# A graph network on one core: the preparation written in another order, and the tables' first evictions moved to ScalarE

## The chip, the cores and the metric

The kernel runs on one core of a Trainium2 chip. The metric is the device time of one launch in microseconds (us); smaller is better. Times given as "the median of the runs" come from unprofiled launches, all others from one launch that the hardware profiler recorded.

## The reference

6250 nodes with 256 features each, and 100000 edges that are sorted by destination. The input is normalised row by row, clipped at zero, and goes through four layers. Each layer adds to every node the sum of the rows of its edges' sources, and then applies three dense maps. The input is added to the result.

```
h = maximum(layernorm(x), 0)
for l in range(3):
    s = h + segment_sum(h[src], dst, num_segments=6250)
    s = relu(s @ W1s[l] + b1s[l])
    s = relu(s @ W2s[l] + b2s[l])
    h = s @ W3s[l] + b3s[l]
s = h + segment_sum(h[src], dst, num_segments=6250)
s = relu(s @ cW1 + cb1); s = relu(s @ cW2 + cb2)      # 256 -> 64
return x + s @ cW3 + cb3
```

## The kernel before

**The main part.** Nodes are kept in 49 blocks of 128. For most pairs of blocks the sums over edges are done as matrix products: a table of edge counts (one byte per pair of nodes) is built once from one-hot matrices, kept in DRAM, and multiplied with the features of all nodes (`agg`, lines L1588 and L1665). The features lie in SBUF as `XY`, split in a high and a low half. For the other blocks of destinations the source rows are fetched one tile at a time (`rows<-table,idx`, L1382, on GpSimd's queue) and summed with small one-hot products (`sums`, L1419). The dense maps are in `mlp`. By linearity W1 is applied ahead of the sum, so that W3 of one layer and W1 of the next are fused into one matrix.

**The preparation** comes before all that and is what the change rewrites. It consists of three Python generators. Each `yield` ends a step, and the order in which the steps are drawn is the order in which each engine gets its instructions; nothing reorders them later. An engine that waits in one instruction holds everything behind it in its own queue.

- `look` finds where the edges of each half block (64 destinations, 98 of them, one to a partition) begin. It loads the first destination of every 128 edges, places each half block roughly (`half`, `at`), fetches a window of `NEAR` destinations for each (`near_i`, L663), and compares that window with 17 thresholds (`less`): 11 comparisons on VectorE (`junk`, L695), 6 on ScalarE (a `Sign` whose results are summed, L698). From `less` it gets the starting edge of every group of 4 destinations (`starts`) and queues 32 gathers of edges (`wd`, `ws`) in the list `asks`. A second, coarser search (`both`, `sel`, `spread`, `part`, L720 to L757) gives the edges of the blocks that are summed row by row, with 14 more gathers (`gd`, `gs`). Then come four rounds in which gathered edges become sources and columns (`hi`, `rel`, `f`, L773 to L779) and are transposed into `clT`, a check that the edges are sorted (`run`, `down`, L794), the flags `wrong`, and the final lists `idx` and `rel` (L826 to L845).
- `normed` normalises the input, two blocks to a step, with lags between its parts: statistics (`moments`, L879, six steps ahead), `scale` (`h`, ScalarE, L899), `turn` (transposes on TensorE, L908, copied to `ht` by ScalarE, L911), `times` (the product with W1, L920, one step after `turn`), `out` (`zs`, L932, every third on ScalarE, else on VectorE), `high` and `low` (`XY`, L936 on ScalarE and L940 on VectorE), `keep` (the store to the table in DRAM).
- `fused` makes the three fused matrices: transposes of W3 (L575, copied by ScalarE, L577), six products (L586, copied by L588), one store each. The bias row comes out of a product whose left side is `b3b`, a copy of the bias spread over 128 columns by GpSimd.

`ask(n)` issues up to `n` of the queued gathers on GpSimd; each waits for the last product of the current step. Before the change, all thresholds, all of `fused` and the coarse search are drawn first, and the steps of `normed` follow with the rest of `look` spread over them.

**After the preparation** the first 12 rounds of table building (`build`) run alone: VectorE makes two one-hot matrices (`lo` and `hi`, L1035), TensorE multiplies them (`bp`, L1076), and the result is evicted as bytes in two pieces, by ScalarE (L1084) and VectorE (L1086) in turn. Then the products of layer 0 start (L1588), fed with casts of the table (`a`, L1549), with the building of the other blocks between them.

## Time and profile before

| | before |
|---|---|
| median of 3 runs | 2129.72 us (2128.97 to 2136.23) |
| the profiled execution's own time | 2135.8 us |
| its span, first to last instruction | 2134.0 us |
| TensorE busy | 2057.4 us, 96% of the span |
| VectorE, ScalarE, GpSimd busy | 937.7, 864.3, 1445.4 us |
| first product of layer 0 starts | 142.70 us after the span's start |

In the views, PE is TensorE, DVE VectorE, ACT ScalarE, POOL GpSimd and SP the engine that issues most transfers; a name with a q (`ACTq`, `SPq`) is the engine's issuing of transfers. A row of a timeline has the start and the duration in us, the engine, the line, the operation, the tile written and the tiles read, the shapes, how often, and in brackets how long the engine stood idle before it and what ended that. A row of windows has, for one stretch of time, the busy time of each engine with its count of instructions, then the granted TensorE clock as a share of full speed, the share of the transfer engines in use, and GB/s.

### The profile page before, as it was taken

Reading aid. Unit: us, or ns where it says so; the run is one execution under the profiler, and the core shown is the slowest. Engines: PE = TensorE matmul, PEld = TensorE weight load, DVE = VectorE, ACT = ScalarE, POOL = GpSimd, SP = SyncE. Lnnn points to the kernel's source line nnn. Section 1 sums busy time; section 2 is a strip of 40 time slices with the busy share of each in tenths; the row PEclk is TensorE's granted clock in tenths of the full one; section 3 lists DMA queues with packets and bytes.
Section 4 is the critical chain, followed back from the end, with each engine's and each line's share of the span. In section 5 each row is a group of like instructions: output and inputs, shape, how many; then the busy total and the mean of one; then the engine's idle time right before and its main releaser. Section 6 shows DMA issues by size and latency. Waiting matters only on the chain.

```text
span 2134.0 us, 33393 instructions
## 1 busy us (share of the span) xinstructions
PE 2057.4 (96%) x12076; PEld 1487.8 (70%) x12076; DVE 937.7 (44%) x2192; ACT 864.3 (41%) x1775; POOL 1445.4 (68%) x1470
## 2 busy tenths in 40 slices
PE   4979999999999999999999999999999999999997
PEld 3756766667667777777776777777776777777675
DVE  7877867667673422222233322222233433333332
ACT  4856655556556522323232433222333432223231
POOL 2727777777774477777776377777776277777773
PEclk9979999999999999999999999999999999999999
DMA  5524545545455655455455554555456555556553
GB/s 157 176 98 139 162 142 153 158 140 164 150 158 152 213 163 155 153 181 164 142 186 167 173 160 148 173 165 169 146 168 195 170 172 181 184 180 194 183 160 119
DMA packets 184901, 347.61 MB, mean 163 GB/s; under 512 B 32446, under 2 KB 118496, under 8 KB 184726
## 3 DMA queue, kind: packets, MB, share of 16 engines
q0 software_dynamic: 68960, 185.41, 29.7%
q1 hardware_dynamic: 113838, 158.12, 22.3%
q8 instruction: 97, 1.59, 0.3%
q10 hardware_dynamic: 1928, 1.85, 0.3%
q14 instruction: 78, 0.64, 0.1%
HBM read 287.98 MB, written 57.26 MB: 162 GB/s over the span
## 4 chain that ended last, share of the span: by engine, by line
PE 88%; DVE 5%; DMA 4%; issue 1%; ACT 1%; POOL 1%; SPq 0%; DVEq 0%; POOLq 0%; ACTq 0%
PE agg L1665 43%; PE agg L1588 16%; PE sums L1419 11%; PE ps L1233 6%; PE ps L1290 6%; PE bp L1076 4%; DMA rows<-table,idx 3%; PE ps L1479 1%; POOL rows L1382 1%; DVE junk L695 1%; PE bp L920 1%; DVE hi L1035 1%; DVE at L1086 1%; PE ps L1245 0%; DMA table<-zs 0%
## 5 line engine op out<-in xcount | busy, mean ns | idle before, releaser
L1382 POOL DMA_INDIRECT rows<-table,idx x1394 | 1387.7, 995 | 611.4 <-issue 220.6
L1665 PE MATMUL agg<-a,XY 128*128 128x512 f32 x4116 | 982.8, 395 | 1.9 <-DVE clT L1600 1.9
L1665 PEld LDWEIGHTS agg<-a,XY 128*128 128x128 f32 x4116 | 764.6, 188 | 209.5 <-issue 45.8
L1565 ACT CAST a<-at 128x512 fp32r<-128x512 uint8 (+1 forms) x542 | 326.9, 616 | 576.9 <-PE agg L1665 543.9
L1565 DVE CAST a<-at 128x512 fp32r<-128x512 uint8 x543 | 242.7, 448 | 552.8 <-PE agg L1665 469.3
L1588 PE MATMUL agg<-XY,a 128*128 128x512 f32 x1470 | 404.9, 409 | 1.3 <-DVE un L1600 0.7
L1588 PEld LDWEIGHTS agg<-XY,a 128*128 128x128 f32 x1470 | 258.9, 189 | 53.7 <-issue 8.7
L1419 PE MATMUL sums<-rows,hot 128*32 128x256 f32 x3772 | 256.0, 385 | 16.2 <-DMA rows<-table,idx 15.0
L1419 PEld LDWEIGHTS sums<-rows,hot 128*32 128x32 f32 x3772 | 112.6, 109 | 142.6 <-issue 53.6
L1549 ACT CAST a<-at 128x512 fp32r<-128x512 uint8 (+2 forms) x362 | 196.7, 574 | 6.5 <-PE agg L1588 6.5
L1084 ACT CAST at<-bp 128x392 uint8<-128x392 f32 x240 | 116.6, 487 | 203.7 <-PE bp L1076 191.0
L1086 DVE CAST at<-bp 128x392 uint8<-128x392 f32 x240 | 135.1, 563 | 138.2 <-PE bp L1076 138.2
L1448 DVE TENSOR_TENSOR u<-u,sums 128x256 f32<-128x256 f32 x82 | 34.3, 419 | 241.8 <-PE agg L1665 226.9
L1076 PE MATMUL bp<-hi,lo 128*128 128x196 bf16 x960 | 127.5, 255 | 11.0 <-DVE hi L1035 10.7
L1290 PE MATMUL ps<-w,h 128*128 128x256 f32 x588 | 133.9, 379 | 1.4 <-ACT h L1236 0.9
L1233 PE MATMUL ps<-h,w 128*128 128x512 f32 (+3 forms) x332 | 133.9, 545 | 0.6 <-DVE zz L1298 0.6
L1035 DVE TENSOR_TENSOR hi<-cols,pairs 128x784 bf16<-128x784 bf16 x240 | 134.3, 560 | 0.0
L1076 PEld LDWEIGHTS <-lo 128*128 128x128 bf16 x960 | 70.6, 99 | 81.9 <-DVE hi L1035 27.8
L1290 PEld LDWEIGHTS ps<-w,h 128*128 128x128 f32 x588 | 111.1, 190 | 18.7 <-ACT h L1236 1.8
L1483 ACT ACTIVATE h<-ps,bias 128x256 f32<-128x256 f32 (+1 forms) x116 | 47.2, 464 | 154.9 <-PE ps L1479 154.9
L1298 DVE TENSOR_TENSOR zz<-ps,w 128x512 f32<-128x512 f32 (+1 forms) x75 | 50.1, 678 | 117.0 <-PE ps L1290 117.0
L1035 DVE TENSOR_TENSOR lo<-lanes,pairs 128x512 bf16<-128x512 bf16 x240 | 100.3, 418 | 1.3 <-ACT pairs L1030 1.3
(171 smaller groups left out, 989.7 us busy)
## 6 DMA issues: line engine op xcount, KB each, us to landing
at<-mat SPq DMA_DIRECT2D x151, 448.0 KB
mat<-at SPq DMA_DIRECT2D x30, 784.0 KB
rows<-table,idx POOLq DMA_INDIRECT x1394
table<-zz SPq DMA_DIRECT2D x72, 256.0 KB
back<-table SPq DMA_DIRECT2D x99, 128.0 KB
xs<-in_x_dram SPq DMA_DIRECT2D x8, 768.0 KB
table<-zs SPq DMA_DIRECT2D x24, 256.0 KB
out_dram<-zz SPq DMA_DIRECT2D x24, 256.0 KB
```

The lines of the kernel that those rows point to most:

```text
L1035: nc.vector.tensor_tensor(o.rearrange("p q (n t) -> p q n t", t=2), values.rearrange("p (n t) -> p n t", t=2)[:, None, :, :].to_broadcast( ...
L1076: mm = nc.tensor.matmul(bp[:, m * HW:(m + 1) * HW], lo[:, q + m, :], hi[:, q + m, :], start=True, stop=True)
L1084: nc.scalar.copy(o, v)
L1086: nc.vector.tensor_copy(o, v)
L1233: mm = nc.tensor.matmul(ps[:mp, :w], weights[l][0][:, c, i * P:i * P + mp], h1[:, c, :w], start=(c == 0), stop=(c == KC - 1))
L1290: mm = nc.tensor.matmul(o, h2[0][:, c, nodes], w3[:, c, :], start=(c == 0), stop=(c == KC - 1))
L1382: got = nc.gpsimd.indirect_dma_start(out=t, out_offset=None, in_=tables[self.l][:, :], in_offset=bass.IndirectOffsetOnAxis(ap=idx[:, o:o + ...
L1419: nc.tensor.matmul(self.sums[m * Q:(m + 1) * Q, :C], self.hot[:, (c - min(rounds)) // 2, m, :], self.rows[g, c + 4 * m], start=(c == ROUND ...
L1549: nc.scalar.copy(a[:, i * m * P:(i + 1) * m * P].rearrange("p (j d) -> p j d", j=m), counts[b][:, j:j + m, :])
L1565: cast(o, at[:, :, d:d + m * P])
L1588: mm = nc.tensor.matmul(agg, a[:, d:d + P], XY[:, j, :], start=(j == 0), stop=(j == NT - 1))
L1665: mm = nc.tensor.matmul(agg[c][:, :w], XY[:, j, o:o + P], a[:, :w], start=(j == 0 and half == 0), stop=(j == NT - 1 and half == 1))
```

## The change

The window `NEAR` shrinks from 1408 to 1280 destinations. Eight comparisons run on VectorE and nine on ScalarE, one or two of each kind in a step of `normed`; after each two such steps the function `settled` works out four groups' `starts` and queues their gathers. The statistics run four steps ahead instead of six, and only the first two of the four early loads of the input are issued ahead of the search. `fused` is drawn one step at a time beside `normed` and loads one layer's weights ahead; the bias is read as a broadcast operand, without `b3b`. The coarse search, its products, the flags and the last lists have steps of their own. In `build`, all evictions of the first 12 rounds are ScalarE's.

```diff
-    NEAR = 11 * P
+    NEAR = 10 * P
...
         load(0)
-        load(1)
         yield
         for l in range(NLAYER):
             w3, w1 = loaded[l]
+            load(l + 1)
...
-            b3b = pool.tile([P, KC, P], F32, name="b3b", bufs=1)
-            nc.gpsimd.tensor_copy(b3b, b3[l][:, :, None].to_broadcast([P, KC, P]))
...
-                    left = w3t[:, k, i * P:(i + 1) * P] if i < KC else b3b[:, k, :]
+                    left = (w3t[:, k, i * P:(i + 1) * P] if i < KC else
+                            b3[l][:, k:k + 1].to_broadcast([P, P]))
...
-        DV = 11
-        for q in range(GSUB + 1):
-            if q < DV:
-                nc.vector.tensor_scalar(junk[:NSUB], near[:NSUB], float(GD * q), None,
-                                        op0=OP.is_lt, op1=OP.add, accum_out=less[:NSUB, q:q + 1])
-            else:
-                nc.scalar.activation(junk2[:NSUB], near[:NSUB], AF.Sign, bias=edge[:NSUB, q:q + 1],
-                                     accum_out=less[:NSUB, q:q + 1])
-                yield
...
+        def settled(q0, q1):
+            odd = slice(q0 + 1 - q0 % 2, q1, 2) if q1 <= GSUB else slice(q0, q1)
+            nc.vector.tensor_scalar(less[:NSUB, odd], less[:NSUB, odd], -0.5, float(NEAR // 2),
+                                    op0=OP.mult, op1=OP.add)
+            nc.vector.tensor_scalar(first[:NSUB, q0:q1], less[:NSUB, q0:q1], at[:NSUB, 0:1], None,
+                                    op0=OP.add)
+            if q1 > GSUB:
+                return
+            nc.vector.tensor_scalar(starts[:, q0:q1], first[:NSUB, q0:q1], float(E - P), None,
+                                    op0=OP.min)
...
+        for q in range(0, GSUB, 2):
+            nc.vector.tensor_scalar(junk[:NSUB], near[:NSUB], float(GD * q), None,
+                                    op0=OP.is_lt, op1=OP.add, accum_out=less[:NSUB, q:q + 1])
+            for k in (q + 1,) if q + 2 < GSUB else (q + 1, q + 2):
+                nc.scalar.activation(junk2[:NSUB], near[:NSUB], AF.Sign, bias=edge[:NSUB, k:k + 1],
+                                     accum_out=less[:NSUB, k:k + 1])
+            yield
+            if q % 4 == 2:
+                settled(q - 2, q + 2)
+        settled(GSUB, GSUB + 1)
...
-        G = 6
+        G, LEAD = 6, 4
...
-            turn_biases()
-            for _ in range(2 * NLAYER):
-                next(looked)
-                next(ahead_w)
-            next(looked)
-            STAGES = (*range(4, 20, 2), 20, 22, 24)
+            STAGES = (*range(16), 17, *range(17, 28))
             for i, _ in enumerate(rows):
-                ask(2)
+                ask(3 if i < 9 else 2)
+                if i == 1:
+                    turn_biases()
+                if i < 2 * NLAYER + 1:
+                    next(ahead_w, None)
                 if i in STAGES:
                     next(looked, None)
...
-                    if step % 2:
+                    if step % 2 or step <= 2 * PRE:
                         nc.scalar.copy(o, v)
                     else:
                         nc.vector.tensor_copy(o, v)
```

Three places show how the instructions move. The first is ScalarE's queue from its first statistics on. Before, the comparisons (`near_i,less`) and the copies of the fused weights (`w3t`, `w_275`, `w_306`) come ahead of the first normalised rows `h`:

```order
L885 ACTIVATE std<-mv,eps 128x6 x2
L550 COPY bias<-ps 128x22
L698 ACTIVATE near_i,less<-near,edge 98x1408
L577 COPY w3t<-ps 128x256 x2
...
L588 COPY w_275<-ps 128x256 x3
...
L588 COPY w_306<-ps 128x256 x3
...
L588 COPY w_333<-ps 128x256 x3
L899 ACTIVATE h<-xs,shift,rstd 128x256 x4
```

In the changed kernel the same queue reads so; L898 is the statistics' root, L912 `scale`, L716 the comparison, L924 `turn`'s copy:

```order
L898 ACTIVATE std<-mv,eps 128x6
L912 ACTIVATE h<-xs,shift,rstd 128x256 x2
L527 DMA w_233<-in_L_gnn_W3s_dram 128x2x256
L527 DMA w1n<-in_L_gnn_W1s_dram 128x2x256
L577 COPY w3t<-ps 128x256 x2
L716 ACTIVATE near_i,less<-near,edge 98x1280
...
L924 COPY ht<-agg 128x512
...
L550 COPY bias<-ps 128x22
L587 COPY w_277<-ps 128x256 x3
```

The rows `h` have moved ahead of all comparisons, and one or two comparisons, one copy of a fused matrix and one pair of `h` now take turns. The second place is the end of the preparation on TensorE. Before, the transposes of the last lists (`wd`, `near`, L835) come ahead of the last transposes of the input and its last product (L920), and ten products into an unused bank (L926) close it:

```order
L920 MATMUL bp<-w_0_114,ht 128x256 x4
L835 MATMUL ps<-ident,wd 128x68 x6
L835 MATMUL ps<-ident,wd 128x17
L835 MATMUL ps<-ident,near 128x68 x6
L835 MATMUL ps<-ident,near 128x17
L908 MATMUL agg<-ident,h 128x128 x2
L920 MATMUL bp<-w_0_114,ht 128x256 x6
L926 MATMUL ps<-XY 128x512 x10
```

In the changed kernel L933 is `times`, L939 the ten products, and L848 the lists' transposes:

```order
L921 MATMUL agg<-ident,h 128x128 x2
L933 MATMUL bp<-w_0_114,ht 128x256 x6
L939 MATMUL ps<-XY 128x512 x10
L848 MATMUL ps<-ident,wd 128x68 x6
L848 MATMUL ps<-ident,wd 128x17
L848 MATMUL ps<-ident,near 128x68 x6
L848 MATMUL ps<-ident,near 128x17
```

The lists' transposes have gone behind all of the input's products. The third place is VectorE at the same end and the start of `build`. Before:

```order
L845 CAST idx<-ps 128x425
...
L932 COPY zs<-bp 128x512
...
L932 COPY zs<-bp 128x256
L940 TENSOR_TENSOR XY<-zs,XY 128x2x256
L940 TENSOR_TENSOR XY<-zs,XY 128x256
L1035 TENSOR_TENSOR lo<-lanes,pairs 128x512
L1035 TENSOR_TENSOR hi<-cols,pairs 128x784
...
L1086 CAST at<-bp 128x49x8
```

In the changed kernel, where L855 and L858 make the last lists, L945 is `out` and L953 `low`:

```order
L945 COPY zs<-bp 128x512
...
L855 TENSOR_SCALAR rel<-ps 128x25x4 x3
L858 CAST idx<-ps 128x425
L945 COPY zs<-bp 128x256
L953 TENSOR_TENSOR XY<-zs,XY 128x2x256
L953 TENSOR_TENSOR XY<-zs,XY 128x256
L1053 TENSOR_TENSOR lo<-lanes,pairs 128x512
L1053 TENSOR_TENSOR hi<-cols,pairs 128x784
```

The last lists, which stood ahead of two `zs`, now stand between the last full pair's `zs` and the last single block's, and in the first 12 rounds of `build` VectorE has only `lo` and `hi` (and one addition), without the `CAST`.

59 lines of the change are left out of this document (34 added, 25 removed).

## The prediction

> **What bounds the kernel now.** I read the page first, then windows over the first 143 us, then the timeline of each engine there. Rows of the page and of the windows:
>
> ```profile
> span 2134.0 us, 33393 instructions
> PE 88%; DVE 5%; DMA 4%; issue 1%; ACT 1%; POOL 1%; SPq 0%; DVEq 0%; POOLq 0%; ACTq 0%
> 0.00:15.20 15.20, 2.92 (x4) 0.96 (x4) 2.69 (x13) 0.00 (x0) 5.92 (x25) 1.00 0.73 221
> 15.20:42.90 27.70, 15.03 (x50) 10.82 (x50) 26.64 (x61) 15.36 (x30) 1.40 (x6) 0.94 0.38 122
> 42.90:66.60 23.70, 21.01 (x112) 16.41 (x111) 21.34 (x73) 17.55 (x38) 18.49 (x18) 0.93 0.55 164
> 66.60:111.70 45.10, 39.39 (x210) 31.12 (x208) 39.44 (x114) 37.19 (x84) 31.93 (x29) 1.00 0.53 158
> 111.70:125.80 14.10, 12.76 (x46) 10.13 (x46) 7.30 (x18) 4.62 (x10) 0.00 (x0) 0.64 0.24 82
> 125.80:142.70 16.90, 9.47 (x50) 5.14 (x50) 16.52 (x39) 7.08 (x18) 7.93 (x8) 0.59 0.45 150
> 200.00:300.00 100.00, 99.61 (x685) 68.94 (x684) 72.98 (x169) 61.12 (x138) 73.86 (x74) 1.00 0.47 142
> ```
>
> TensorE carries 88% of the chain, and in the sample from 200 to 300 us it is busy 99.61 of 100 us. The code there is unchanged (eviction alternates as before after round 12), so an earlier start of the products moves the end by as much. What the change can win or lose lies before 142.7 us. There VectorE is the third number of busy time: 26.64 of 27.70 us, later 39.44 of 45.10, and 16.52 of 16.90 in the first rounds of `build`. Its idle time up to 125.8 us is 125.8 less the 97.4 us that the first five windows add up to, 28.4 us: 12.5 at the front, 6.8 at the end (111.7 to 125.8), 9.1 between.
>
> ```profile
> 15.56 0.42 DVE L879 BATCH_NORM_STATS2 stats<-xs 128x6 f32<-128x256 f32 x1
> 22.80 0.94 DVE L689 TENSOR_SCALAR near<-near_i,low 98x1408 f32<-98x1408 int32 x1
> 9.08 0.63 DVE L654 TENSOR_SCALAR_CACHE_REDUCE junk<-ps,low 98x391 bf16<-98x391 f32 x1 [1.83 <-PE ps L652]
> 23.77 1.62 DVE L695 TENSOR_SCALAR_CACHE_REDUCE junk<-near 98x1408 bf16<-98x1408 f32 x1
> 25.44 1.62 DVE L695 TENSOR_SCALAR_CACHE_REDUCE junk<-near 98x1408 bf16<-98x1408 f32 x1
> 23.83 1.47 ACT L698 ACTIVATE near_i<-near,edge 98x1408 bf16<-98x1408 f32 x1 [1.43 <-POOL b3b L579]
> 43.48 2.08 ACT L899 ACTIVATE h<-xs,shift,rstd 128x256 f32<-128x256 f32 x4
> 48.31 0.57 ACT L911 COPY ht<-agg 128x512 f32<-128x512 f32 x1
> ```
>
> The input's first statistics start at 15.56, the first `h` only at 43.48: TensorE's 25 products of the input stand behind the thresholds. One comparison takes VectorE 1.67 us from start to start.
>
> **Part by part. VectorE's work.** Eleven comparisons of 1.67 us are 18.4 us. The slope between 391 and 1408 columns, (1.62-0.63)/1017, is 0.97 ns a column, so 1280 columns cost 1.54 us, eight 12.3. That removes 6.1 us. `settled` repeats three small instructions four times and two of them once more; the first, the last and what followed them:
>
> ```profile
> 41.95 0.17 DVE L701 TENSOR_SCALAR less<-less 98x6 f32<-98x6 f32 x1
> 42.42 0.17 DVE L706 TENSOR_SCALAR starts<-first 98x16 int32<-98x16 f32 x1
> 42.50 0.21 DVE L720 TENSOR_SCALAR both<-first,since 98x1 f32<-98x1 f32 x1
> 45.31 1.00 PE L738 MATMUL ps<-both,near_i 98*68 98x6 f32 x14 [2.13 <-DVE near_i L735]
> ```
>
> The three take 0.55 us (41.95 to 42.50); four times, and 0.4 more, in place of once, is 2.1 us more. VectorE's work falls by 4.0, from 97.4 to 93.4 us. `b3b` goes from GpSimd, which is busy 1.40 us from 15.2 to 42.9; that is on no path.
>
> **The front.** Behind the list of first destinations comes the first block of the input (0.79 MB). These rows are the hardware queue's packets from 6 to 8 and from 8 to 10 us; what it moved earlier is mostly the list:
>
> ```profile
> q1 hardware_dynamic: 450, 0.46, 73.5%
> q1 hardware_dynamic: 732, 0.73, 109.1%
> ```
>
> The block is in at about 9. Its first two tiles' statistics now come in front of the rough search; twelve tiles and their roots lie between 15.56 and 22.80, 0.6 us each, so the window's gather starts 1.2 us later. On SP's queue `run` goes behind two input loads and ahead of two, with more than 20 us to spare, and ScalarE issues one layer's weights less there. Up to the window 4.2 MB are queued (five loads and the window); at 0.365 MB a microsecond they are in at 8+3.7/0.365, about 18 to 19, when VectorE has done ten tiles. So `h` starts at about 16 instead of 43.48, as soon as six tiles and their root are done, and `near` at 19 instead of 22.80.
>
> **Steps 0 to 8.** In these nine steps VectorE has, from 19: `near` (0.9), eight comparisons (12.3), 16 tiles with roots (9.6), `settled` (2.7), the coarse search (2.8, from 42.50 to 45.31) and nine `zs` or `XY` of some 0.6: 33.7 us, up to 52.7. ScalarE's queue is longer, and its order is fixed. A comparison costs 1.34 there (1.47 less 128 columns at the 1 ns that lies between the 1408 columns of its row and the 512 of `ht`, 0.57). Up to its last comparison ScalarE has 16 `h` at 0.52 (8.3), 7 `ht` (4.0), 9 comparisons (12.1), 15 copies for the fused weights at 0.37 (5.6), and 13 short ones at some 0.45 (5.9: `zs`, `XY`, roots, issues of loads): 35.9 us. It starts at 16, waits 1 us for `near` and by my estimate 2 more for TensorE, because the copies of each fused matrix stand ahead of the next comparison:
>
> ```profile
> L588 ACT COPY w<-ps 128x256 f32<-128x256 f32 x9 | 3.4, 373 | 5.3 <-PE ps L586 5.2
> 25.70 3.78 PE L586 MATMUL ps<-w1n,w3t 128*128 128x256 f32 x8 [2.56 <-ACT w3t L577]
> 39.99 1.99 PE L586 MATMUL ps<-w1n,w3t 128*128 128x256 f32 x8 [1.28 <-ACT w3t L577]
> 47.48 3.32 PE L920 MATMUL bp<-w,ht 128*128 128x256 f32 x8
> 51.07 1.89 PE L920 MATMUL bp<-w,ht 128*128 128x256 f32 x8
> ```
>
> That puts the last comparison at about 55, and with some 4.5 us of VectorE's work behind it (`settled`, coarse search, one `XY`) step 8 ends at 59.5 instead of 52.7: VectorE waits some 7 us for ScalarE here. What was one wait at the front becomes several short ones.
>
> **Step 9 to the end.** Before, VectorE at 66.6 had done the same `zs` and `XY`. What it still had was 39.44+7.30 = 46.7 us of work. After step 8 the changed kernel has this and 6.8 more: four tiles of statistics (2.1), the coarse search's last part (13 instructions like L706's, 2.0), the first of the four rounds on edges (four instructions over 512 columns, by the slope 0.67 each, 2.7). 59.5+53.5 = 113.0 without waits. The gathers do not bind: they start in step 3, near 32, instead of behind `starts` at 42.42, and two or three fit a step, by GpSimd's 18 in the 23.7 us from 42.9. At the end stand these rows:
>
> ```profile
> 111.43 0.34 DVE L828 SCALAR_TENSOR_TENSOR wd<-colf,skip,wd 17x128 f32<-17x128 f32 x1
> 116.06 1.10 PE L835 MATMUL ps<-ident,wd 68*128 68x68 f32 x7
> 122.66 2.62 PE L926 MATMUL ps<-XY 128*128 128x512 f32 x10
> 123.39 0.42 DVE L932 COPY zs<-bp 128x256 f32<-128x256 f32 x1
> 125.80 0.40 ACT L1030 COPY pairs<-clT 128x64 bf16<-128x64 bf16 x2 [1.55 <-DMA table<-zs]
> ```
>
> Before, 14.4 us pass from the last `wd` to `pairs`, because two pairs of blocks follow the lists. Now the products come before the lists, but the ten spare products (2.62) and the lists' transposes stand ahead of the last `zs`: 2.62 and the first half of the transposes, 0.6 to 1.1, about 3.3 us of wait for VectorE. The last store costs about 1 us beyond VectorE's end (2.0 from the last `zs` to `pairs`, one of them filled with `XY`). With 1.5 us, an estimate, for the late steps in which TensorE's transposes and its 1.89 us of products outlast VectorE, `pairs` starts at 118.8 instead of 125.8: **7.0 us less**. Below, it could be 1 (every handoff longer by half a microsecond), above, 14 (ScalarE never waits).
>
> **The first rounds of building.**
>
> ```profile
> 128.18 0.42 DVE L1035 TENSOR_TENSOR lo<-lanes,pairs 128x512 bf16<-128x512 bf16 x1
> 128.52 0.56 DVE L1035 TENSOR_TENSOR hi<-cols,pairs 128x784 bf16<-128x784 bf16 x1
> 129.00 0.56 DVE L1086 CAST at<-bp 128x392 uint8<-128x392 f32 x1
> 129.47 0.41 DVE L1035 TENSOR_TENSOR lo<-lanes,pairs 128x512 bf16<-128x512 bf16 x1
> 129.13 0.84 PE L1076 MATMUL bp<-hi,lo 128*128 128x196 bf16 x4 [0.79 <-DVE hi L1035]
> 129.68 0.48 ACT L1084 CAST at<-bp 128x392 uint8<-128x392 f32 x1 [0.98 <-PE bp L1076]
> 142.70 2.07 PE L1588 MATMUL agg<-XY,a 128*128 128x512 f32 x4 [0.64 <-ACT a L1549]
> ```
>
> A round takes 1.29 us, all VectorE's (`lo` 0.34, `hi` 0.48, eviction 0.47). Without the eviction VectorE needs 0.82, TensorE 0.84, ScalarE two evictions of 0.48. The floor is 0.84; with both evictions in series, 1.0, which I take because each waits for its own products: 12 x 0.29 = **3.5 us less**, between 0 and 5.3.
>
> **The sum.** 7.0 + 3.5 = 10.5 us. The profiled execution took 2135.8 us, 2134.0 in its span and 1.8 around it, and would take 2125.3. It lies 6.1 us above the median of the runs, 2129.72, which would become 2119.2.
>
> [...] TensorE's products ran at half pace at 25.70 (3.78 against 1.99 at 39.99) and again at 47.48 (3.32 against 1.89), with the granted clock at 0.94 and 0.93 over the two windows. The change spreads matmuls thinly over steps 0 to 8. [...] By the trace alone I have put the half pace only on the first fused matrix and the first product.
>
> **The rivals.**
>
> - *ScalarE does not bind* (17%). Steps 0 to 8 go at VectorE's pace, end at 52.7, and the median is 6.8 us lower, 2112.4. For it: ScalarE was busy only 37.19 of 45.10 us in the long window. Against: 35.9 us are queued behind a start at 16.
> - *The preparation ends hardly sooner* (17%). ScalarE and TensorE wait for one another in each of the steps, and only `build` gains, with 0 to 1 us from the preparation: 2126. For it: six such handoffs lie in the queue.
> - *The half clock lasts* (11%); this one ends on the other side. Seven products and two fused matrices in steps 0 to 8 at the lower pace cost 7 x 1.43 + 2 x 1.8 = 13.6 us, less some 3 that TensorE has free; four more steps add 3.9 (1.43 each, less what VectorE leaves free). That is 14.5, and the kernel takes 2133.7, slower than now. It turns slower once about eight steps run so.
> - *The eviction is no gain* (5%). ScalarE's pairs of evictions and casts take 1.29 us a round, and the change to `build` does nothing: 2122.7.
>
> **How the numbers follow.** My sum has 50%; its own range, from the bounds of the ScalarE waits and of the round, is 2114 to 2125, with half of it below 2119.1. About 0.5%, 10.6 us, is what a measurement of this kernel tells from no change: faster means below 2119.1, slower above 2140.4. Faster is half of the sum's 50% and the first rival, 0.42. Slower needs the half clock over still more steps, 0.05. The rest, 0.53, is within. The range 2111 to 2130 takes in all but the half clock and the edges.
>
> **What would show it.** Right: the first `h` near 16 us, VectorE idle for ScalarE several times between 25 and 60, the gathers from about 32, `pairs` at about 119, rounds of about 1.0 us with ScalarE's evictions back to back, the first product of layer 0 near 132. Wrong: eight products of a pair above 3 us in more than two steps, VectorE busy without gaps from 19 on, rounds still 1.29, or a layer 0 that gives the time back.

## The result

The changed kernel takes 2130.95 us (median of 12 runs, 2128.12 to 2133.63) beside 2132.26 us of the kernel before (12 runs, 2127.64 to 2138.86): a ratio of 0.9992, 95% interval 0.9982 to 1.0002. That is no change that can be told. Two later comparisons gave 0.9997 (0.9987 to 1.0007) and 0.9996 (0.9986 to 1.0005). The forecast of 2119.2 us is missed by some 12 us, and the range ends 1 us below the measured value. The experiments ran in groups, each beside the kernel before. In three groups a disturbance made every kernel 10 to 12% longer; those runs are compared only within their group.

The profiled execution of the changed kernel took 2130.1 us, close to its median. These are its page's rows on the span, TensorE and the chain:

```profile
span 2128.3 us, 33390 instructions
PE 2059.1 (97%) x12076; PEld 1487.3 (70%) x12076; DVE 926.4 (44%) x2185; ACT 871.5 (41%) x1793; POOL 1442.2 (68%) x1467
PE 88%; DVE 2%; DMA 2%; issue 1%; ACT 1%; POOL 1%; SPq 0%; DVEq 0%; ACTq 0%; POOLq 0%
```

VectorE's share of the chain fell from 5% to 2%: the preparation did get shorter. The same windows as before the change (the fifth now ends where `pairs` starts, the sixth where the first product of layer 0 starts; the clock, a share of full speed, is the third number from the end):

```profile
0.00:15.20 15.20, 4.15 (x8) 1.54 (x8) 4.79 (x22) 0.01 (x1) 3.63 (x13) 1.00 0.74 215
15.20:42.90 27.70, 20.32 (x85) 15.45 (x86) 18.34 (x56) 19.82 (x42) 8.03 (x20) 1.00 0.57 171
42.90:66.60 23.70, 19.04 (x94) 14.53 (x93) 20.70 (x63) 21.04 (x43) 14.34 (x16) 0.93 0.62 180
66.60:111.70 45.10, 39.91 (x205) 31.66 (x204) 43.14 (x126) 35.30 (x81) 29.51 (x27) 0.96 0.43 131
111.70:119.98 8.28, 5.03 (x31) 4.09 (x30) 5.46 (x16) 1.41 (x4) 0.00 (x0) 0.88 0.25 85
119.98:134.04 14.06, 10.00 (x51) 5.49 (x51) 12.40 (x29) 11.44 (x30) 8.89 (x8) 0.50 0.56 180
200.00:300.00 100.00, 99.61 (x678) 68.21 (x677) 72.85 (x169) 60.12 (x136) 73.12 (x74) 1.00 0.51 153
```

VectorE falls from 26.64 to 18.34 us in the second window, and TensorE rises from 15.03 to 20.32: the products of the input now start there. From `pairs` to the first product it takes 14.06 us instead of 16.90. Rows of the timelines of ScalarE, VectorE, GpSimd and TensorE in the changed kernel:

```profile
17.49 0.60 ACT L912 ACTIVATE h<-xs,shift,rstd 128x256 f32<-128x256 f32 x1 [0.70 <-DVE shift L905]
21.22 0.89 DVE L689 TENSOR_SCALAR near<-near_i,low 98x1280 f32<-98x1280 int32 x1 [2.19 <-DMA near_i<-in_dst_dram,at_i]
30.99 0.17 DVE L699 TENSOR_SCALAR less<-less 98x2 f32<-98x2 f32 x1 [3.53 <-ACT near_i L716]
34.76 0.99 POOL L609 DMA_INDIRECT wd<-in_dst_dram,starts  x1 [17.05 <-DVE stats L892]
39.99 0.69 DVE L953 TENSOR_TENSOR XY<-zs,XY 128x512 fp32r<-128x512 f32 x1 [2.83 <-ACT XY L949]
56.05 1.36 ACT L716 ACTIVATE near_i<-near,edge 98x1280 bf16<-98x1280 f32 x1
116.08 1.08 DVE L855 TENSOR_SCALAR rel<-ps 128x100 bf16<-128x100 f32 x6 [1.74 <-PE ps L848]
119.98 0.39 ACT L1048 COPY pairs<-clT 128x64 bf16<-128x64 bf16 x2 [1.54 <-DMA table<-zs]
121.73 3.52 ACT L1102 CAST at<-bp 128x392 uint8<-128x392 f32 x8 [1.36 <-PE bp L1094]
134.04 2.08 PE L1606 MATMUL agg<-XY,a 128*128 128x512 f32 x4 [1.03 <-ACT a L1567]
```

`h` starts at 17.49 instead of 43.48 (in the trace of before the last thing it reads, the first `shift`, was there at 22.28, and `h` stood behind the comparisons and copies in ScalarE's queue), `pairs` at 119.98 instead of 125.80, the first product at 134.04 instead of 142.70. Eight evictions of the build steps take ScalarE 3.52 us back to back, so a round of two takes 0.88 to 0.92 us. The start of the products has come 8.7 us forward. The two profiled spans differ by 5.7 us, and the medians by 1.3.

**Where the rest went in the two traces.** From all matmul records and the record of the granted clock one can split the time from the first layer-0 product to the last: TensorE's idle time between products, the work done at half clock, and the remainder. Half of the work at half clock is counted as loss: in the trace of after the products `agg<-a,XY` follow one another in 427 ns at a granted clock of 0.50 and in 227 at 1.00 (medians). The remainder is 1948 to 1951 us in each of the eleven traces of the table below, so all else differs by 3 us at most. Between the two traces the products start 8.7 us earlier, idle time is 1.7 less (26.2 for 27.9), half-clock work 6.9 more (19.0 for 12.1, a loss of 3.4), and from the last product to the span's end it takes 1.2 us longer (8.1 for 6.9). That gives 5.8; the spans differ by 5.7.

Two places show the half clock. Windows of 10 us from the first product on and of 15 us around the change from layer 0 to layer 1, first of before, then of after:

```profile
142.70:152.70 10.00, 10.00 (x49) 7.39 (x50) 7.14 (x19) 7.34 (x17) 1.07 (x2) 0.85 0.04 16
688.00:703.00 15.00, 13.15 (x54) 9.40 (x53) 4.84 (x11) 4.59 (x10) 0.00 (x0) 1.00 0.60 198
```

```profile
134.04:144.04 10.00, 10.00 (x46) 7.22 (x47) 5.71 (x15) 6.75 (x16) 0.95 (x1) 0.78 0.00 0
680.00:695.00 15.00, 13.15 (x44) 9.22 (x43) 4.68 (x11) 4.32 (x9) 0.00 (x0) 0.89 0.55 180
```

The granted clock is 0.78 against 0.85 at the start, 0.89 against 1.00 at the layer's change, with equal busy time (13.15) but 44 instead of 54 products done. The timeline of TensorE at that change, before and after:

```profile
695.82 1.21 PE L1665 MATMUL agg<-a,XY 128*128 128x512 f32 x4 [1.85 <-DVE clT L1600]
696.87 3.62 PE L1290 MATMUL ps<-w,h 128*128 128x256 f32 x16
```

```profile
687.78 1.95 PE L1683 MATMUL agg<-a,XY 128*128 128x512 f32 x4 [1.85 <-DVE clT L1618]
689.52 4.53 PE L1308 MATMUL ps<-w,h 128*128 128x256 f32 x16
```

The same wait of 1.85 us, and behind it the same four products take 1.95 us instead of 1.21.

**What the trace of before stands for.** That execution took 2135.8 us, 5.0 above the median of the 52 runs of the kernel before that stand beside the first two groups of experiments (2130.8). A second trace of it, below, was of an execution of 2137.8. So the medians lie closer than the traces do.

### The profile page after: what moved, and what is told of

It reads as the page before. It is cut to its first block, busy times and chain, and to the rows that moved or that the text cites. A ratio compares the mean times of both kernels' runs of the same rounds, so it can differ in the third digit from the quotient of the medians.

```text
span 2128.3 us, 33390 instructions
## 1 busy us (share of the span) xinstructions
PE 2059.1 (97%) x12076; PEld 1487.3 (70%) x12076; DVE 926.4 (44%) x2185; ACT 871.5 (41%) x1793; POOL 1442.2 (68%) x1467
## 3 DMA queue, kind: packets, MB, share of 16 engines
q10 hardware_dynamic: 1928, 1.85, 0.3%
## 4 chain that ended last, share of the span: by engine, by line
PE 88%; DVE 2%; DMA 2%; issue 1%; ACT 1%; POOL 1%; SPq 0%; DVEq 0%; ACTq 0%; POOLq 0%
PE agg L1683 44%; PE agg L1606 16%; PE sums L1437 11%; PE ps L1251 6%; PE ps L1308 6%; PE bp L1094 4%; DMA rows<-table,idx 2%; PE ps L1497 1%; POOL rows L1400 1%; PE ps L1263 1%; PE ps L1243 0%; DVE hi L1053 0%; ACT at L1102 0%; DVE at L1104 0%; DVE lo L1053 0%
## 5 line engine op out<-in xcount | busy, mean ns | idle before, releaser
L1102 ACT CAST at<-bp 128x392 uint8<-128x392 f32 x252 | 120.9, 488 | 197.1 <-PE bp L1094 183.7
L1104 DVE CAST at<-bp 128x392 uint8<-128x392 f32 x228 | 128.7, 565 | 139.5 <-PE bp L1094 139.5
```

Of the source, the lines that this page charges most:

```text
L1102: nc.scalar.copy(o, v)
L1104: nc.vector.tensor_copy(o, v)
```

## The experiments

Two theories at first. A: the 8.7 us are won and the medians are off by scatter; the end moves with the start of the products. B: something behind the preparation gives a shift of the start back.

**A known delay, on both kernels.** Nine repeats of a comparison on VectorE behind all of the preparation (10.06 us together in both traces):

```diff
                 nc.vector.tensor_copy(o, ps[:, :left[NQ]])
         yield
+        yield
+        ...
+        for _ in range(9):
+            nc.vector.tensor_tensor(down, run[:, 1:EC + 1], run[:, :EC], OP.is_lt)
```

Put into the kernel before:

> The kernel before, with nine idle-work comparisons of 1.08 us each put on VectorE behind the whole preparation, ahead of the first one-hot tile: the first layer-0 product is to start some 8.4 us later, near 151, and everything behind it is unchanged. Theory A (the end moves with the start of the products; the 8.7 us were won, and the small difference of the medians is scatter): about 8 us slower than the kernel before, near 2140. Theory B (something behind the preparation gives a shift of the start back, at a layer's end or in the clock): at most 2 us slower, near 2133.

Measured: 2140.85 us beside 2130.66, ratio 1.0045 (1.003 to 1.0059). Put into the kernel after:

> The kernel after, with the same nine comparisons of 1.08 us on VectorE behind the preparation: its first layer-0 product is to start near 142.5, where that of the kernel before starts, with all other parts of the change kept. Theory A: 8 us slower than the kernel after and so 6 to 7 us slower than the kernel before, near 2139, if the change costs something behind the preparation; equal to the kernel before, near 2132, if the medians of before and after are off by scatter. Theory B: within 2 us of the kernel after, near 2132.

Measured: 2135.33 us, ratio to the kernel before 1.0026 (1.0012 to 1.004). **Parts of the change.** Only the eviction edit in the kernel before, and all of the change without it:

```diff
-                    if step % 2:
+                    if step % 2 or step <= 2 * PRE:
                         nc.scalar.copy(o, v)
```

> The kernel before, with only the one-line edit that puts the evictions of the first 24 build steps on ScalarE. The rounds are to fall from 1.29 to about 0.92 us, so that the first layer-0 product starts some 3 to 4 us earlier, near 139. Theory A: 3 to 4 us faster than the kernel before, near 2129. Theory B: within 1 us of it, near 2132.

Measured: 2127.86 us, ratio 0.9983 (0.9971 to 0.9994).

> The kernel after without the one-line edit of the build evictions: pairs still near 120.0, the rounds back at 1.29 us, the first layer-0 product near 137 to 138. Theory A: 3 to 4 us slower than the kernel after, near 2134. Theory B: within 1 us of the kernel after, near 2131.

Measured: 2130.75 us, ratio 0.9999 (0.9988 to 1.001). The first product in the traces of the four, in this order:

```profile
151.64 0.80 PE L1594 MATMUL agg<-XY,a 128*128 128x512 f32 x1 [0.64 <-ACT a L1555]
```

```profile
143.50 2.07 PE L1612 MATMUL agg<-XY,a 128*128 128x512 f32 x4 [1.03 <-ACT a L1573]
```

```profile
140.27 2.07 PE L1588 MATMUL agg<-XY,a 128*128 128x512 f32 x4 [1.03 <-ACT a L1549]
```

```profile
137.24 2.08 PE L1606 MATMUL agg<-XY,a 128*128 128x512 f32 x4 [0.64 <-ACT a L1567]
```

On the old preparation the end follows the start: 2.4 us earlier gives 2.8, 8.9 us later gives 10.2. (The first of these is a weak sign: unchanged, the kernel before moves its start by 2.1 us from one trace to the next, as shown below.) With the new preparation it doesn't. `all_but_evict` starts its products 5.5 us before the kernel before and ends level with it; `after_late` starts them 0.8 us later and ends 4.7 later. Theory A as it stands has fallen. B has fallen on the old preparation, where a delay is not absorbed; on the new one 9.5 us of delay (143.50 for 134.04) cost 4.4 to 5.3 us against the medians of the unchanged kernel in other groups (2130.05 to 2130.95). Measured from the one trace of before, some 4 to 7 us are lost behind the first product wherever the new preparation is in front.

**The clock.** The next theories. C: what lies behind the preparation is the same for all but for waits and half-clock windows. D: the start of the products moves from run to run. E: the clock costs nothing there. Both kernels unchanged, for more traces:

> The kernel before once more, unchanged, for a second trace. In the first trace TensorE, from its first layer-0 product to its last, waits 27.9 us and works 12.1 us at half clock (6.05 us lost), and that execution lies 3.5 to 5 us above the median of its kernel. Theory C (what lies behind the preparation is the same for both kernels but for waits and half-clock windows, which differ from run to run): a run near 2130.7 has a first product near 142.7 again and idle time plus half of the cold time near 29 instead of 34. Theory D (the start of the products moves from run to run): the first product of a run near 2130.7 lies near 138.

Measured: 2130.57 us (0.9993, 0.9982 to 1.0005), the traced execution 2137.8, first product at 140.62. An execution so far above the median doesn't tell C from D.

> The kernel after once more, unchanged, timed beside the others. In its first trace TensorE waits 26.2 us and works 19.0 us at half clock after its first product at 134.04. Theory C: first product within 0.5 us of 134.0, idle time plus half of the cold time 32 to 37, median near 2129.5. Theory D: the first product lies near 138 in a run near the median.

Measured: 2130.16 us (0.9997, 0.9987 to 1.0007), the traced execution 2129.6, first product at 133.26: idle time 26.6 and half the half-clock work 9.75, 36.4 together, as C has it, though the start lay 0.74 us from 134.0 where C allowed 0.5. The start of the products does move from run to run, by 2 us on the kernel before and by 3.5 on the changed one (136.72 in a third trace), but not by the 8 us that separate the kernels, so D alone doesn't do. Then the changed kernel with spare products, which nobody reads, in TensorE's idle time between its last product of the preparation and layer 0:

```diff
+        still = ps_m.tile([P, W], F32, name="ps")
+        for _ in range(18):
+            nc.tensor.matmul(still, XY[:, 1, :P], XY[:, 0, :], start=True, stop=True)
         yield
...
+                    if step % 2 == 0 and step <= 2 * PRE:
+                        still = ps_m.tile([P, W], F32, name="ps")
+                        nc.tensor.matmul(still, XY[:, 1, :P], XY[:, 0, :], start=True, stop=True)
                     if step % 2 or step <= 2 * PRE:
```

> The kernel after with spare products that nobody reads, to keep TensorE's clock up until layer 0: eighteen of 128x512 behind the lists' transposes, where TensorE idles 4.5 us, and one behind every second step of the first 24 build steps. The half clock from 117.9 to 138.4 is to go. Theory C: the first product stays near 134 and the 3 to 6.3 us at half clock behind it vanish, 1.5 to 3.2 us, near 2128; with the waits unchanged. Theory E (the clock costs nothing there, the loss is in waits on gathers): no change, near 2130.

Measured: 2122.56 us (5 runs, 2122.0 to 2124.56), ratio to the kernel before 0.9963 (0.9949 to 0.9976): 7.6 us below `after_again` of the same group, more than was expected. Windows of its trace from `pairs` to the first product, the 10 us behind it, and the layer's change:

```profile
120.97:134.04 13.07, 10.92 (x70) 6.75 (x68) 11.88 (x29) 10.90 (x30) 9.10 (x8) 1.00 0.59 188
134.04:144.04 10.00, 9.99 (x57) 7.48 (x58) 7.13 (x18) 7.95 (x18) 2.03 (x3) 1.00 0.20 68
679.00:694.00 15.00, 13.15 (x56) 9.48 (x55) 3.92 (x10) 5.37 (x12) 0.00 (x0) 1.00 0.55 180
```

The first product starts at 134.04, as in the first trace of after, but the clock is full: 57 products in the first 10 us instead of 46. That speaks against E: with the start unmoved, the spare products are worth 7.6 us. Not all of it is shown to be the clock's. The span of this trace is 7.1 us shorter than that of `after_again`, though its products start 0.8 us later: the half clock gives 5.1 us of it (9.3 us of such work for 19.5) and idle time 1.6, and some 1.3 are in the remainder. Of the 5.1, 1.7 come from the layer's change, where this execution kept the clock (1.00 over the 15 us) and that of `after_again` did not (0.89); the end of this section sorts the traces by what went before.

> The kernel after_warm with the ten spare products that stand ahead of the lists' transposes moved behind them, 28 there in all. VectorE's wait of 1.74 us for the transposes is to go, so pairs starts some 2 us sooner, near 118, and the first product near 132. Theory C: 2 us faster than after_warm, near 2126. Theory E: near 2130.

Measured: 2121.94 us, ratio 0.9961 (0.9946 to 0.9975); no different from `after_warm`. Rows of its trace:

```profile
116.14 8.22 PE L861 MATMUL ps<-XY 128*128 128x512 f32 x28 [1.06 <-DVE rel L855]
118.78 0.40 ACT L1047 COPY pairs<-clT 128x64 bf16<-128x64 bf16 x2 [1.51 <-DMA table<-zs]
124.19 0.51 PE L1093 MATMUL bp<-hi,lo 128*128 128x196 bf16 x4
```

`pairs` came forward as expected, but the 28 spare products ran into a half-clock window, took 8.22 us (eighteen took 4.34 in `after_warm`) and held the first build step until 124.19. The first product started at 135.69, later than in `after_warm`, and in the two traces only the smaller half-clock work behind it (5.4 us for 9.3) evened that out.

**The account of all undisturbed traces.** Worked out as described above (us; half clock counts the busy time behind the first product at half clock; the last column runs from the start of the last product):

| trace | its time | first product | idle | half clock | to the end |
|---|---|---|---|---|---|
| before | 2135.8 | 142.70 | 27.9 | 12.1 | 6.9 |
| before_again | 2137.8 | 140.62 | 28.0 | 18.0 | 7.2 |
| before_late | 2139.9 | 151.64 | 24.9 | 8.5 | 6.8 |
| evict_only | 2132.5 | 140.27 | 25.1 | 18.1 | 6.2 |
| after | 2130.1 | 134.04 | 26.2 | 19.0 | 8.1 |
| after_again | 2129.6 | 133.26 | 26.6 | 19.5 | 8.0 |
| after_third | 2126.5 | 136.72 | 25.6 | 8.2 | 8.3 |
| after_late | 2138.8 | 143.50 | 27.9 | 17.5 | 6.3 |
| all_but_evict | 2129.4 | 137.24 | 26.0 | 19.6 | 6.3 |
| after_warm | 2122.6 | 134.04 | 25.0 | 9.3 | 8.1 |
| after_warm_moved | 2121.4 | 135.69 | 24.1 | 5.4 | 8.3 |

The two executions of the changed kernel near its median (after, after_again) worked 19 us at half clock behind the first product. For the kernel before there is no undisturbed trace of a usual execution, since both traced ones took 5 and 7 us more than its median; nearest comes `before_late`, 0.9 us below its kernel's median. The nine comparisons took 10.06 us, and VectorE waited 0.43 us for `pairs` behind them where it had waited 1.34: less this delay of 9.15 us its first product would start at 142.5. Against it the two traces of after start 8.8 us earlier, idle 1.5 us more, lose 5.4 us more to the half clock and end 1.2 us later behind the last product: 0.7 us are left of 8.8. The medians of the three comparisons lie 1.0 to 1.5 us apart. That account rests on one trace that stands in for another, and it leaves `after_third` out. Over the whole table the four traces with the old preparation have 8.5 to 18.1 us at half clock (mean 14.2), the five with the new one and no spare products 8.2 to 19.6 (mean 16.8): a difference in loss of 1.3 us, well inside the scatter.

**What the clock's record says besides.** Directly behind the first product the half clock lasts 3.1 and 3.3 us in the two traces of before and 4.4, 4.8 and 3.9 us in the three of after, a loss of 1.6 against 2.2 us. The rest lies far behind, near 690, 1160, 1650 and 2105 us, and not every execution has it at all four. The mean granted clock is on record for every run: it amounts to 44.2 us at half clock in a whole execution of the kernel before (67 runs) and 43.2 us of the changed one (34 runs). So the change does not add half-clock time; at most it moves some of it from the preparation to behind the first product. Ahead of that product, counted from some 30 us on, where the record begins, the traces of before have 31.1 and 24.0 us, those of after 22.9, 12.3 and 16.6. But both traces of before had some 51 us in all, 7 more than usual. If these 7 lay in the preparation, usual executions of both kernels lose the same behind it (means of 15.1 and 15.6 us at half clock in the traces); if they lay behind it, the changed kernel loses some 4 us more. By this estimate the clock's share of what the changed kernel loses behind its first product is anything from 0 to 4 us.

**Does the kernel before gain as much from spare products?** If so, the clock takes the same from both and the account is wrong (theory C); if it loses little there, the change loses what it wins (theory F). C1 and C2 ask again where usual executions of the kernel before start their products.

```diff
-                for _ in range(10):
+                for _ in range(16):
                     nc.tensor.matmul(still, XY[:, 1, :P], XY[:, 0, :], start=True, stop=True)
...
+                    if step % 2 == 0 and step <= 2 * PRE:
+                        still = ps_m.tile([P, W], F32, name="ps")
+                        nc.tensor.matmul(still, XY[:, 1, :P], XY[:, 0, :], start=True, stop=True)
                     if step % 2:
```

> The kernel before with spare products, read by nobody, to keep TensorE's clock up from the last products of the input until layer 0: sixteen instead of ten at the end of the preparation and one behind every second step of the first 24 build steps. Theory C (both kernels lose the same to the clock behind the preparation, on average): some 6 to 8 us faster than the kernel before, near 2124, with the first product near 141. Theory F (the change itself is what lets the clock fall: the kernel before loses little there): at most 2 us faster, near 2129, so that the warm kernels differ by the 7 to 8 us that the preparation won.

> The same, with the evictions of the first 24 build steps on ScalarE as in the change; the rest of the preparation is that of the kernel before. First product near 137.5. Theory C: near 2121, about 3 us faster than before_warm and as fast as after_warm plus 3. Theory F: near 2126.

> The kernel before, unchanged, for a third trace: both traces so far are of executions (2135.8 and 2137.8 us) well above the median of its runs, 2130.8. Theory C1 (the start of the products is stable and the 3 to 5 us above the median lie behind it, in waits and half-clock work): first product between 140.5 and 143, and in a run near 2131 idle time plus half of the cold time near 28. Theory C2 (the half clock inside the preparation moves the start from run to run): in a run near 2131 the first product lies near 137 to 139, with fewer half-clock windows before 60 us.

> The kernel before, unchanged, for a fourth trace; expected as for the third.

These four, the three that follow and `before_warm_3` with `after_warm_short` are the disturbed groups: kernels took 2340 to 2400 us. In all nine traces TensorE stood idle for 84 to 100 us that the profile puts down to `issue`, waiting for nothing that it shows; in the trace of before that is 0. What caused it is not known. The window from 200 to 300 us of the kernel before under the disturbance (`before_fifth`):

```profile
200.00:300.00 100.00, 90.84 (x621) 61.85 (x620) 70.64 (x164) 57.30 (x133) 67.18 (x67) 1.00 0.46 136
```

TensorE is busy 90.84 us instead of 99.61. Measured against the kernel before of the same group (2389.19 us): `before_warm` 0.9991 (0.9976 to 1.0006), `evict_warm` 0.997 (0.9955 to 0.9985). Their first products started at 144.37 and 142.66, 3 and 5 us later than expected. The two traces of the kernel before (2390.5 and 2388.5 us) start the products at 144.32 and 144.93 and tell nothing of a usual execution elsewhere.

> The kernel before with spare products that keep TensorE's clock up until layer 0, as in before_warm. Theory C (the clock costs both kernels the same behind the preparation): 6 to 8 us faster than the kernel before, near 2124, and after_warm_2 no more than 2 us faster still. Theory F (the kernel before loses little to the clock there; the change loses what it wins): at most 2 to 3 us faster, near 2129.

> The changed kernel with the spare products, as in after_warm (2122.6 there), now beside before_warm_2. Both theories: near 2122.5, 8 us below the kernel before. Theory F: 6 to 8 us below before_warm_2, the whole of what the preparation won; theory C: within 2 us of it.

> The kernel before, unchanged, for a trace of a usual execution. If it falls near 2131: theory C1, first product between 140.5 and 143 and idle time plus half of the cold time behind it near 28 instead of 34 to 37; theory C2, first product near 137 to 139.

Measured, beside a kernel before of 2361.62 us: `before_warm_2` 0.9987 (0.9971 to 1.0003), `after_warm_2` 0.9939 (0.9918 to 0.9961), `before_fifth` 1.0014 (0.9998 to 1.0029). `after_warm_2` is 11.9 us below `before_warm_2` (2348.36 for 2360.28), more than the 6 to 8 of theory F and far from the 2 of C; their first products start at 133.50 and 149.22. `before_fifth` came nowhere near 2131 and decides nothing between C1 and C2.

> The kernel before with the spare products, as in before_warm, in the hope of a chip without the stalls. Theory C (the clock costs both kernels the same behind the preparation): 6 to 8 us faster than the kernel before, near 2124. Theory F (the kernel before loses little there): at most 3 us faster, 2128 or more.

Measured: 0.9979 (0.9963 to 0.9995) of a kernel before of 2390.9 us. Three times the spare products gave the kernel before 0.1 to 0.2%, and two of the three intervals reach 1. They did what they were put there for: between `pairs` and the first product the half clock lasts 3.4 us in each of the three traces, and 14 us in the three traces of the unchanged kernel (`before_third` to `before_fifth`). That speaks for F, but weakly: under the disturbance TensorE works 72 to 103 us at half clock all through the kernel, and the changed kernel without spare products was not run in these groups, so what they give to it there is not known.

**The version that the runs point to.** The spare products behind the transposes go into a PSUM tile that is free at once, eighteen of them, and none stand ahead:

```diff
-            if s == len(pairs) - 1:
-                still = ps_m.tile([P, W], F32, name="ps")
-                for _ in range(10):
-                    nc.tensor.matmul(still, ...)
+            if s == len(pairs) - 1:
+                spare_ps.append(ps_t.tile([P, W], F32, name="agg"))
...
+        still = spare_ps[0]
+        for _ in range(18):
+            nc.tensor.matmul(still, XY[:, 1, :P], XY[:, 0, :], start=True, stop=True)
```

> The changed kernel with the spare products cut to what keeps the clock up: none ahead of the lists' transposes (VectorE's wait of 1.7 us there goes), eighteen behind them into a PSUM tile that is free at once, one behind every second step of the first 24 build steps. In after_warm_moved pairs started at 118.8 but the 28 spare products held the first build step back to 124.2; here it is to start near 120.2, the first product near 131.7 and the clock full. Theories C and F alike: 2 us below after_warm, near 2120.5, 10 us below the kernel before.

Measured, in the group of `before_warm_3`: 0.9915 (0.9898 to 0.9932) of the kernel before, 20 us less, the best ratio of all, and 16.8 us below `before_warm_3`. Rows of its trace:

```profile
114.39 4.37 PE L861 MATMUL agg<-XY 128*128 128x512 f32 x18
118.16 0.41 ACT L1051 COPY pairs<-clT 128x64 bf16<-128x64 bf16 x2 [1.50 <-DMA table<-zs]
131.00 1.20 PE L1612 MATMUL agg<-XY,a 128*128 128x512 f32 x4 [0.93 <-ACT a L1573]
```

The first product starts at 131.00, with the clock full (four products in 1.20 us). It has been timed only under the disturbance; the expected 2120.5 us elsewhere were not measured.

> The changed kernel, unchanged, for a third trace. First product near 133.5. Theory F (the clock takes most of what its preparation wins): 0 to 4 us below the kernel before, on a chip with the stalls as on one without. Theory C: 6 to 8 us below it where the stalls leave the clock less to lose.

Measured, undisturbed: 2130.05 us, 0.9996 (0.9986 to 1.0005). Its traced execution took 2126.5 us, 3.6 below the median, though its first product came late, at 136.72: it met the half clock for only 8.2 us.

**Where the clock fell at the change from layer 0 to layer 1.** In the record of the granted clock every stretch at one value lasts a whole number of times 3.41 us, but for the last one, which ends with the record: 1, 3, 1, 18, 3, 2, 5 and 299 times up to 1166.35 us in the trace of before, 9, 1, 3, 1, 12, 6 and 161 times up to 687.95 in that of after. Below, a window is one such step of 3.41 us. The position of the windows under the kernel differs from execution to execution: the record begins at 29.71 us in the one trace and at 29.18 in the other. The wait of 1.85 us at the change from layer 0 to layer 1 is the same in all twenty traces. Where it lay whole inside one window (beginning 0.11 to 1.39 us behind the window's start, nine traces), TensorE was 46% busy in that window and the next one was at half clock; in the trace of after the wait began at 685.93, in the window from 684.54, and the clock was 0.50 from 687.95 to 691.37. Where it was split over two windows (beginning 1.62 to 3.41 us behind the start, eleven traces), both were busier, if only by a little (46.0% for 45.8% in the closest case), and the clock stayed full; in the trace of before the wait began at 693.97, in the window from 691.90, which was 61% busy. It is nine of nine and eleven of eleven, with four of the nine on the kernel before or on its warm variants and five with the new preparation or the eviction edit. Elsewhere the border is less sharp: over all windows of the eleven undisturbed traces the clock fell behind windows of up to 48%, and behind four of 55 to 69% in which transposes ran (in the trace of after, 65% from 114.51 us), which is not shown to be the cause; it stayed full behind four windows of 45 to 47%.

## Why the prediction was wrong

- **The step that failed** is the one that carried every case: "The code there is unchanged (...), so an earlier start of the products moves the end by as much." The code is unchanged, and a sample from 200 to 300 us is as busy as before (99.61), but outside such samples lie 24 to 28 us of idle time and 5 to 20 us at half clock, and they are not the same from one execution to the next. The runs showed this instead: the start came 8.7 us forward, the traces' spans differ by 5.7, because the half clock took 3.4 and the tail 1.2 while idle time gave 1.7 back, and the medians differ by 1.3, because the trace of before was an unusually long execution. `all_but_evict`, 5.5 us ahead at its first product and level at the end, says the same; `after_warm`, 7.6 us faster with the start unmoved, shows that the start alone does not set the end. How much of it the new preparation itself brings about is not shown: 5.4 us by the stand-in trace, 0 to 4 by the clock's record. The text had named "a layer 0 that gives the time back" as what would make it wrong, and had put no case and no chance on it.
- **The clock as a rival** was weighed, but only inside the preparation, for thin matmuls at half pace. There it cost little: behind the first 30 us, for which there is no record, the trace of after has the half clock from 59.90 to 63.31, from 73.55 to 76.97 and from 117.93 us on, and `h` to `pairs` went nearly as summed. The granted clock in the windows up to 42.90 us says little about it, 0.94 before and 1.00 after: in both traces the record begins at 29 to 30 us, and the half pace that the prediction saw at 25.70 lies ahead of that. What the sum had no term for is the half clock from `pairs` on, where TensorE has 10.00 busy of 14.06 us at a clock of 0.50 all the time, and what is left of it behind the first product.
- **The sum's terms** were nearly right. `h` at 17.49 (forecast 16), `near` at 21.22 (19; VectorE waited 2.19 us for the window's gather), the gathers from 34.76 (32), ScalarE's last comparison up to 57.4 (55), VectorE's waits for ScalarE up to 60 us 7.7 us together (7), the longest 3.53 and 2.83, `pairs` 5.8 us earlier (7.0). From `pairs` to the first product 2.8 us less (3.5): the rounds became shorter than forecast, 0.9 us for 1.0, but behind the last one the first product waits 1.03 us for a cast, 0.64 before. Together 8.7 of 10.5.
- **The base of the sum.** It was made against a trace of 2135.8 us and carried over to the median as it stood. That median was of 3 runs, 2129.72; with 12 it is 2132.26. Of the 5.7 us between the two traces, 3.5 are how far the trace of before lay above this median, and 0.8 how far the trace of after lay below its own. Both undisturbed traces of the kernel before were of executions 5 to 7 us above the median, so part of what lies in the trace's 142.7 us and behind it was not there in usual ones. The evidence for how much in which is one stand-in trace; it stays open.
- **What also stays open:** whether usual executions with the old preparation meet fewer half-clock windows behind it than with the new one, and why. The position of the windows differs between executions of one kernel (over the 15 us around the layer's change the clock was 0.89, 0.89 and 1.00 in the three traces of after), and with three undisturbed traces of one kernel and two of the other it can't be told from their scatter (8.2 to 19.5 us). The tail behind the last product takes 6.9 to 7.2 us in the undisturbed traces of the kernel before and 8.0 to 8.3 in those of the changed one, but 6.3 in `after_late` and `all_but_evict`; its cause wasn't looked for.

## What to carry to other kernels

A stage on the critical path that is made shorter need not move the end by as much. Here the start of the products came 8.7 us forward and the medians by 1.3, and spare products in the binding engine's idle time ahead of them were worth 7.6 us (`after_warm` against `after_again`): look at what the binding engine does in the idle time ahead of it, and try to fill that time. Before a sum is made against a trace, find out where its execution lies among the runs: here one trace was 5 us above the median, as much as half of the gain in question. A known delay put at the same place is a cheap test of whether the end follows the start.

## What the runs showed of the hardware

- In nine of twenty traces TensorE's wait of 1.85 us at the layer's change lay whole in one window of 3.41 us of the clock's record, TensorE was 46% busy in that window, and in all nine the clock was at half in the next one. By an estimate, half of 3.41, each of them cost some 1.7 us; in the traces of after and before the twenty products behind the wait took 6.27 us with such a window and 4.67 without. In the eleven traces where the wait was split over two windows the clock stayed full.
- In the changed kernel the clock stayed at 0.50 from 119.98 to 134.04 us, though TensorE was busy 10.00 of 14.06 us there, in products of 196 columns. Two of the record's windows in there were 92 and 90% busy (from 121.3 and 124.8 us; 0.919 and 0.901) and brought no change; a window of the same products that was 0.925 busy in `after_again` (from 121.0 us) and one of 0.930 in `evict_only` (from 129.5) were followed by the full clock. With eighteen spare products of 512 columns, put where the clock was still full (they took 4.34 us together), and one in every second step it was 1.00 in `after_warm` from 120.97 to 134.04 us.
- An execution with 1 us more at half clock (from each run's mean granted clock) took 0.40 us longer, over 52 runs of the kernel before; half of the half-clock time would be 0.5. By this fit two thirds of the variance of this kernel's runs (2125.6 to 2138.1 us) go with the clock; over the 34 runs of the changed kernel it is 0.29 us, and somewhat less than half.
